# Second pass of a channel attention and dilated attention kernel: q of two groups in quarters of TensorE, in banks shared with the position taps, and two scaled taps summed by accumulating transfers

## The chip, the cores and the metric

The kernel runs on one core of a Trainium2 chip, in float32 with a few bfloat16 operands. The metric is the device time of one execution in microseconds (us), the median of several. The engines are called as in the profile: PE (TensorE matmuls), PEld (its weight loads), DVE (VectorE), ACT (ScalarE), POOL (GpSimd), SP (SyncE, which here only issues transfers).

## What is computed

The input `x` is 4 images of 192 channels and 128 x 128 pixels. Layer 0 is a channel attention: it ends in a per-channel mix of `v`, a gate and `x`, projected by a 1x1 convolution. Layer 1, which the change touches, takes the result `x` and does:

```python
pe = conv3x3_depthwise(x, pos_w)                  # nine taps a channel
x = x + pe + pos_b
qkv = einsum('oc,bchw->bohw', qkv_w, x)           # 192 -> 576 channels
# three groups of 64 channels (2 heads of 32), dilation 1, 2, 3:
scores = einsum('bnpd,bnpdk->bnpk', q, k_3x3)     # nine neighbours, reflected at the edges
attn = softmax(scores * 32**-0.5)
out_g = einsum('bnpk,bnpkd->bnpd', attn, v_3x3)
out = einsum('oc,bchw->bohw', proj_w, concat(out_1, out_2, out_3))
```

## The kernel before

There are three stages: a projection of `x` (`project`), the channel attention's matrices (`channel_attention`), and the second pass (`second_pass`), which does the last product of layer 0 and all of layer 1. Only the second pass is changed.

It works on blocks `n` of 4 image rows of two images at once: 64 blocks, of 512 pixels per image. Channels 0 to 127 of the two images lie in two tiles side by side, `hboth` (128 partitions, rows, 2 images, width); channels 128 to 191 of both images share one tile of 128 partitions, 64 for each (`HALVES`). For a block, in order:

- `h_product` (L803) and `h_evict` (L807): the output of layer 0 goes into rings of rows, `hboth` and `hring[2]`.
- The position taps of the first 128 channels: `centre` (L846) has ACT write the middle tap with the bias into the PSUM tile `pa` (two banks, one buffer), seven taps on DVE add to it (`tap`, L858; one operand is `hboth`, the other is `pa`), the last of them writes `y` in SBUF. The ninth tap, number 3, is scaled by ACT (`moved`, L870) and added to `y` by POOL (`moved_sum`, L875).
- The same taps for the last 64 channels: nine scaled copies on ACT (`side`, L882), added row by row by two accumulating transfers that POOL issues (`side_rows`, L894), and then by two POOL additions (L902, L905) into `y2`.
- `kv_product` (L945, L948) multiplies keys and values; ACT copies them into rings of rows, `kring` and `vring` (`kv_evict`, L958), with the reflected edges (`reflect`, L962, L963).
- `query` gives q of one group at a time in the bank `q` (one buffer): first two matmuls of 128x64 side by side (L1003, one for each image, which land in the two halves of the partitions), then one of 128x128 (L1000) whose weights `wq2` hold the 64-channel matrix twice on the diagonal and zeros elsewhere.
- `prod` (L1011) on DVE multiplies q with three windows of the key ring at a time, nine of them for a block; `pick_sums` (L1022) sums over the 32 channels of a head on PE; then the softmax (L1065 to L1110), whose weights a transposing transfer (L1110) turns.
- `expand` (L1146) spreads the weights over channels on PE into two banks, `term` (L1152) multiplies them with the value ring on DVE, `term_sum` (L1155) adds up on POOL, with four buffers for terms; `out_product` (L1164, L1168), `out_evict` (L1171) and `store` end the block.

The order of all instructions on every engine is computed when the kernel is built. `Schedule` keeps a list of operations, each with an engine, a rank (a due time in blocks), an estimated cost in us, what it comes after, a latency to other engines and, for PE, the shape of its setting. `hold` says that a buffer is taken by one operation and free after others, with as many in use at once as the pool has buffers. `order` then simulates the engines: a free engine takes the ready operation of lowest rank. The result is a fixed order in which each engine runs its instructions on the chip, waiting at each for what it needs. A changed cost, rank or buffer count therefore changes the written order of everything.

PSUM has eight banks: `pc` 2, `ex` 2, `q` 1, `pa` 2 (one tile), `sc` 1.

The planning of q and its products reads:

```python
t0 = n + 4.65
for g in range(NG):
    a = add("PE", t0 + (NT * g + 0.1) / 27, 0.86, (query, n, g, 0), [y[2]], COLS)
    b = add("PE", t0 + (NT * g + 0.11) / 27, 0.86, (query, n, g, 1), [a] + y[3], FULL)
    for ty in range(3):
        op = add("DVE", t0 + (NT * g + 3 * ty + 0.5) / 27, 1.75, (prod, n, g, ty), [b])
    hold("q", a, *mine)
```

Here `y[2]` is the finished `y`, `y[3]` that and `y2`.

Of the kernel before, what the change touches and what calls it, by code (L numbers as in the profile page):

```python
# [19 lines left out]
G = 64  # L20
NG = 3
# [13 lines left out]
class Schedule:  # L35
# [9 lines left out]
    def add(self, engine, rank, cost, run, after=(), shape=None, latency=LATENCY):  # L45
        op = dict(engine=engine, rank=rank, cost=cost, run=run, shape=shape, latency=latency, seq=len(self.ops))
        op.update(after=list(after), first=[], users=[], issued=[])
        self.ops.append(op)
        return op

    def hold(self, pool, bufs, first, last):

        self.pools.setdefault((pool, bufs), []).append((first, last))
# [130 lines left out]
    return t.rearrange("p (r w) -> p r w", w=W)  # L184


FULL, COLS, ROWS, QUADS = "128x128", "128x64", "64x128", "128x32"
HALVES = [slice(0, G), slice(G, 128)]
EXTRA = 2 * B * CH0 + B
SM = EXTRA + B * 2 * CH0  # L190
XV = 8
GATE = "wl wl2 dwl fc1T bfc1 fc2T bfc2 eye wprojT".split()
SECOND = "wp1 wq1 wq2 wkv wkv2 wo wo2 posw posb pick order spread".split()
AROUND = (0, 1, 2, 6, 7, 8, 3, 5)


# [550 lines left out]
def second_pass(tc, x, w2, xv_p, mix1, mix2, biases, v_dram, v2_dram, out):  # L747
# [4 lines left out]
    with ExitStack() as ctx:  # L752
# [3 lines left out]
            tc,  # L756
            "p2",
            dict(
                xv=XV, y=3, y2=3, prod=3, middle=2, side=1, moved=1, term=4, acc=4, o=3, s_sb=1, e=2, mx=2, sm=2, e_sb=2,
            ),  # L760
            dict(pc=2, ex=2, q=1, pa=1, sc=1),
            dict(xv=xv_p),
        )
        add, hold, tile_of, tiles = stage.schedule.add, stage.hold, stage.tile, stage.tiles
# [74 lines left out]


        by_row = lambda a: a.rearrange("p r b w -> p (r b) w")

        def centre(n):
            at = n * RB % RING
            to, of = tile_of("pa", ("pa", n), (128, RB, 2, W)), hboth[:, at : at + RB, :, 1 : W + 1]
            nc.scalar.activation(  # L846
                by_row(to), by_row(of), AF.Identity, bias=posb[:, 0:1], scale=posw[:, 0, 4:5]
            )
# [15 lines left out]
                    ALU.add,  # L864
                )

        def moved(n, t):
            to = tile_of("moved", ("moved", n), (128, RB, 2, W))
            at = n * RB % RING
            nc.scalar.activation(  # L870
                by_row(to), by_row(hboth[:, at : at + RB, :, t % 3 : t % 3 + W]), AF.Copy, scale=posw[:, 0, t : t + 1]
            )

        def moved_sum(n):
            nc.gpsimd.tensor_add(tiles["y", n], tiles["y", n], tiles.pop(("moved", n)))  # L875

        def side(n, ty, tx):

# [28 lines left out]
        def plan_conv(n):  # L907
            prev = first = add("ACT", n + 2, 1.25, (centre, n), latency=0.3)
            for m in range(2):
                read("h", m, n, 0, first)  # L910
            for j, t in enumerate(AROUND[:7]):
                prev = add("DVE", n + 2 + (j + 0.9) / 8, 1.28, (tap, n, t, j == 6), [prev])
                for m in range(2):
                    read("h", m, n, t // 3 - 1, prev)
            hold("pa", first, prev)
            two = prev
            mv = add("ACT", n + 2.5, 1.2, (moved, n, AROUND[7]))
            for m in range(2):
                read("h", m, n, 0, mv)
            both = add("POOL", n + 2.9, 2.4, (moved_sum, n), [mv, two])  # L920
            hold("moved", mv, both)
            firsts, sums = {}, []
            for j, ty in enumerate((1, 0, 2)):
                for tx in range(3):
                    sd = add("ACT", n + 2 + 0.3 * j + 0.08 * tx, 0.72, (side, n, ty, tx), firsts.get(ty, [])[-1:])
                    read("h", 2, n, ty - 1, sd)
                    firsts.setdefault(ty, []).append(sd)
                if j:
                    after = [firsts[1][-1], firsts[ty][-1], *sums[-1:]]
                    sums.append(add("POOL", n + 2.25 + 0.3 * j, 1.2, (side_rows, n, ty), after, latency=6.0))  # L930
                    hold("side", firsts[ty][0], sums[-1])
# [23 lines left out]
        def kv_evict(n, pair, im, e, kind, g):  # L955

            _, _, rows, pad = ring_rows(n, kind, g)
            nc.scalar.copy(rows[HALVES[im], :, pad : pad + W], rows3(tiles["pkv", n, pair, im])[HALVES[e]])  # L958

        def reflect(n, kind, g):  # L960
            _, _, rows, pad = ring_rows(n, kind, g)
# [31 lines left out]
            for at, length, o in runs(n, dy, size, True):  # L993
                yield ring[g][:, at : at + length, dx : dx + W], slice(o * W, (o + length) * W)

        def query(n, g, j):

            q = tile_of("q", ("q", n, g)) if j == 0 else tiles["q", n, g]
            if j:
                mm(q, wq2[:, g, :], tiles["y", n, 2], start=False, stop=True)  # L1000
                return
            for im in range(2):
                mm(rows3(q[HALVES[im]]), wq1[:, g * G : (g + 1) * G], tiles["y", n, im], start=True, stop=False)  # L1003

        def prod(n, g, ty):

# [23 lines left out]
        def plan_scores(n, y):  # L1030
            t0 = n + 4.65
            prods, used, picks = [], [], []
            for g in range(NG):
                a = add("PE", t0 + (NT * g + 0.1) / 27, 0.86, (query, n, g, 0), [y[2]], COLS)
                b = add("PE", t0 + (NT * g + 0.11) / 27, 0.86, (query, n, g, 1), [a] + y[3], FULL)
                used += [a, b]
                mine = []
                for ty in range(3):
                    op = add("DVE", t0 + (NT * g + 3 * ty + 0.5) / 27, 1.75, (prod, n, g, ty), [b])
                    read("k", g, n, (ty - 1) * (g + 1), op)  # L1040
                    mine.append(op)
                hold("q", a, *mine)
                prods += mine
            for row in range(7):
                of = prods[4 * row // 3 : min(4 * row + 3, NG * NT - 1) // 3 + 1]
                op = add("PE", of[-1]["rank"] + (2.5 + 0.1 * row) / 27, 0.86, (pick_sums, n, row), of, QUADS)
                op["after"] += picks[-1:]
                picks.append(op)
            for k, op in enumerate(prods):
                hold("prod", op, picks[(3 * k + 2) // 4])  # L1050
            return used, picks
# [131 lines left out]
        def plan_mixed(n, w):  # L1183
            t0 = n + 6.1
            sums, spreads = [], []
            for g in range(NG):
                exs, prev = [], None
                for t in range(NT):
                    u = t0 + (NT * g + t) / 27
                    exs.append(add("PE", u - 0.6 / 27, 0.25, (expand, n, g, t), [w], FULL))  # L1190
                    tm = add("DVE", u + 0.7 / 27, 0.62, (term, n, g, t), exs[-1:])
                    read("v", g, n, (t // 3 - 1) * (g + 1), tm)
                    hold("ex", exs[-1], tm)
                    if t == 0:
                        first = prev = tm
                        continue
                    prev = add("POOL", u + 1.2 / 27, 1.27, (term_sum, n, g, t), [tm, prev])
                    hold("term", tm, prev)
                spreads += exs
                sums.append((first, prev))  # L1200
            hold("e_sb", w, *spreads)
            used = []
            for m in range(2):
                ops = []
                for g in range(NG):
                    after = [sums[g][1]] + ops[-1:]
                    ops.append(
                        add(
                            "PE",
                            n + 7.25 + 0.07 * m + 0.01 * g,  # L1210
                            0.86,
                            (out_product, n, m, g),
                            after,
                            FULL if m else ROWS,
                        )
                    )
# [28 lines left out]
def _shapes_only():  # L1245
# [6 lines left out]
    pick[np.arange(128), QR + np.arange(128) // HD1] = 1  # L1252
    order = np.zeros((128, NS), f)
    for col in range(NS):
        order[col // 4 % 4 * 32 + col // 16 * 4 + col % 4, col] = 1
    spread = np.zeros((3, NT, 4, NT, 4, HD1), f)
    for t in range(NT):
        for h in range(4):
# [117 lines left out]
```

## Time and profile before

| | us |
|---|---|
| time, median of 3 runs (lowest to highest) | 4568.01 (4566.82 to 4569.73) |
| the profiled execution's own time | 4564.56 |
| its span, first to last instruction | 4562.7 |
| busy: PE, DVE, POOL, ACT | 4416.8, 3907.4, 3354.2, 2506.2 |

The stages can be told apart in the busy tenths: up to about 840 us the projection, up to about 1650 the channel attention, then the second pass, which is even from about 1800 to 4400 us and drains at the end. A row of a group gives its line, engine and operation, output and inputs, sizes, count, then busy us, mean ns of one, and the idle time of the engine ahead of it with what ended it. A float32 matmul appears as two records. The clock granted to TensorE was 0.987 of full speed over the span, and 1.00 in the even part of the second pass. Nearly all records of an even stretch are there; a few per cent of the matmuls and some other records are missing.

### The profile page before, as it was taken

The page shows a single profiled execution, that of the slowest core. Times are in us where ns is not written, and L with a number is a line of the kernel's source. Part 1 is how long each engine was busy: PE and PEld are TensorE (multiplying, and loading weights), DVE is VectorE, ACT ScalarE, POOL GpSimd, SP SyncE. Part 2 cuts the span into 40 slices and gives each one's busy share as a digit, 9 for nine tenths or more (in the row PEclk, how much of TensorE's full clock was granted, in tenths as well). Part 3 has the DMA queues.
Part 4 walks back from the last instruction along what each step waited for, and adds up shares of the span by engine and source line. Part 5 has one row for each costly group of instructions (what it writes and reads, how often), then busy time and mean ns, then how long its engine had stood idle before and what let it go on. Part 6 is the DMA issues. An engine that isn't in the chain of part 4 may idle for free.

```text
span 4562.7 us, 64190 instructions
## 1 busy us (share of the span) xinstructions
PE 4416.8 (97%) x20608; PEld 1602.8 (35%) x20608; DVE 3907.4 (86%) x5556; ACT 2506.2 (55%) x4794; POOL 3354.2 (74%) x3343
## 2 busy tenths in 40 slices
PE   9999999899999989999999999999999999999986
PEld 3333333345544532333333333333333333333321
DVE  7998889755455547899999999999999999999996
ACT  7888888633233345555555555555555555555531
POOL 6777788611111115888989999998998989999897
PEclk9999999999999989999999999999999999999997
DMA  8777787678677734443444443444434444344311
GB/s 271 241 242 232 244 256 242 192 164 178 150 167 169 167 89 97 99 99 97 101 98 93 105 103 91 106 96 101 101 90 108 98 100 101 92 109 99 78 44 28
DMA packets 483951, 608.93 MB, mean 133 GB/s; under 512 B 136528, under 2 KB 318364, under 8 KB 483616
## 3 DMA queue, kind: packets, MB, share of 16 engines
q1 hardware_dynamic: 464160, 504.94, 40.6%
q0 software_dynamic: 19456, 99.89, 11.3%
q8 instruction: 166, 2.72, 0.3%
q14 instruction: 169, 1.38, 0.1%
HBM read 277.72 MB, written 201.33 MB: 105 GB/s over the span
## 4 chain that ended last, share of the span: by engine, by line
PE 71%; DVE 14%; issue 6%; POOL 6%; DMA 2%; ACT 1%; POOLq 0%; SPq 0%; DVEq 0%; ACTq 0%
PE pc L576 11%; PE ph L803 9%; PE pu L293 7%; PE ex L1146 6%; PE sc L1022 6%; DVE prod L1011 5%; DVE term L1152 5%; POOL acc L1155 4%; PE pu L298 4%; PE gram L648 4%; PE po L1168 3%; PE po L1164 3%; PE pkv L945 3%; PE pu L426 2%; PE q L1000 2%
## 5 line engine op out<-in xcount | busy, mean ns | idle before, releaser
L1155 POOL TENSOR_TENSOR acc<-acc,term 128x512 f32<-128x512 f32 x1536 | 1977.4, 1289 | 211.9 <-DVE term L1152 135.5
L1152 DVE TENSOR_TENSOR term<-ex,vring 128x512 f32<-128x512 f32 (+2 forms) x1596 | 1007.3, 661 | 65.8 <-PE ex L1146 38.9
L1011 DVE TENSOR_TENSOR prod<-q,kring 128x1536 f32<-128x1536 f32 (+1 forms) x600 | 1008.3, 1686 | 31.7 <-ACT kring L963 13.8
L363 POOL TENSOR_TENSOR v_True<-v_True,side 128x512 f32<-128x512 f32 (+1 forms) x512 | 647.9, 1267 | 168.8 <-ACT side L352 141.1
L340 DVE SCALAR_TENSOR_TENSOR pa<-vboth,dwv,pa 128x1024 f32<-128x1024 f32 (+1 forms) x448 | 574.3, 1282 | 76.8 <-ACT pa L333 54.3
L1146 PE MATMUL ex<-e_sb,spread 108*128 108x512 bf16 x1728 | 596.2, 387 | 45.2 <-DVE acc L1152 21.3
L858 DVE SCALAR_TENSOR_TENSOR pa<-hboth,posw,pa 128x1024 f32<-128x1024 f32 (+1 forms) x384 | 489.5, 1275 | 59.0 <-ACT pa L846 45.1
L576 PE MATMUL pc<-u,band 64*64 64x508 f32 (+1 forms) x4608 | 517.5, 590 | 1.4 <-ACT ring L322 1.4
L563 POOL COPY band<-band 64x384 f32<-64x384 f32 x192 | 96.7, 504 | 561.3 <-DMA band<-in_bands 484.8
L1022 PE MATMUL sc<-prod,pick 128*32 128x512 f32 x3456 | 484.1, 607 | 4.1 <-DVE e L1079 2.8
L589 DVE BATCH_NORM_STATS2 stats<-pc 128x6 f32<-128x128 f32 x1440 | 303.3, 283 | 141.3 <-ACT conv L585 141.1
L1146 PEld LDWEIGHTS <-spread 108*128 108x128 bf16 x1728 | 149.0, 98 | 723.7 <-issue 692.2
L945 PE MATMUL pkv<-y,wkv 128*128 128x512 f32 x768 | 389.0, 618 | 8.1 <-ACT kring L958 2.5
L882 ACT ACTIVATE side<-hring,posw 128x512 f32<-128x512 f32 x512 | 335.2, 710 | 102.1 <-DMA side<-side 79.8
L803 PE MATMUL ph<-xv,mix 128*128 128x512 f32 (+1 forms) x1024 | 383.4, 606 | 5.4 <-DMA xv<-v_dram 4.9
L585 ACT COPY conv<-pc 128x512 f32<-128x512 f32 x384 | 211.4, 587 | 295.4 <-PE pc L576 288.8
L293 PE MATMUL pu<-xt,wx 128*128 128x512 f32 x768 | 365.3, 612 | 7.6 <-DMA xt<-in_x 7.6
L352 ACT ACTIVATE side<-ring,dwv 128x512 f32<-128x512 f32 (+1 forms) x512 | 350.6, 736 | 15.1 <-POOL v_True L363 14.3
L958 ACT COPY kring<-pkv 64x512 f32<-64x512 f32 x384 | 223.2, 581 | 221.7 <-PE pkv L948 210.5
L576 PEld LDWEIGHTS pc<-u,band 64*64 64x64 f32 x4608 | 188.4, 133 | 302.3 <-issue 282.1
L1171 ACT COPY o<-po 128x512 f32<-128x512 f32 x192 | 106.2, 588 | 304.5 <-PE po L1164 203.8
L958 ACT COPY vring<-pkv 64x512 f32<-64x512 f32 x384 | 223.4, 582 | 45.4 <-PE pkv L948 35.7
(164 smaller groups left out, 5961.0 us busy)
## 6 DMA issues: line engine op xcount, KB each, us to landing
qk_dram<-us SPq DMA_DIRECT2D x192, 512.0 KB
u<-qk_dram SPq DMA_DIRECT2D x384, 256.0 KB
side<-side POOLq DMA_DIRECT2D x124, 768.0 KB, 5.8
xt<-in_x SPq DMA_DIRECT2D x64, 512.0 KB
v_dram<-v_False SPq DMA_DIRECT2D x64, 512.0 KB
xv<-in_x SPq DMA_DIRECT2D x128, 256.0 KB
xv<-v_dram SPq DMA_DIRECT2D x128, 256.0 KB
out<-o SPq DMA_DIRECT2D x128, 256.0 KB
```

The costliest lines, as they stand in the source:

```text
L293: mm(pu, wx[:, mt * 128 : (mt + 1) * 128], tiles["xt", n][:, im, :], start=True, stop=False)
L340: nc.vector.scalar_tensor_tensor(by_row(to[:, o : o + length]), by_row(vboth[:, at : at + length, :, t % 3 : t % 3 + W]), dwv[:, 0, t : t ...
L363: nc.gpsimd.tensor_add(v[:, rows, :], v[:, rows, :], z[:, rows, :])
L576: nc.tensor.matmul(pcs[e][r * G : (r + 1) * G, :, to], band[at, e, c, dx, :], u[at, e, c, :].rearrange("p (b w) -> p b w", w=W)[:, :, of], ...
L803: mm(to, w[:, cols], tiles["xv", n, j, im], start=j == 0, stop=j == 2)
L858: nc.vector.scalar_tensor_tensor(by_row(to[:, o : o + length]), by_row(hboth[:, at : at + length, :, t % 3 : t % 3 + W]), posw[:, 0, t : t ...
L945: mm(rows3(tile_of("pc", key)), w, tiles["y", n, im], start=True, stop=False)
L1011: nc.vector.tensor_mul(to[:, :, px].rearrange("p t (r w) -> p t r w", w=W), q.unsqueeze(1).to_broadcast([128, 3, *q.shape[1:]]), three,)
L1022: mm(sc[quad * 32 : (quad + 1) * 32, :], pick[:, QR - 4 * row : QR - 4 * row + 32], tiles["prod", n, k // NT, k % NT // 3][:, k % 3, :], s ...
L1146: mm(rows3(tile_of("ex", ("ex", n, g, t))), spread[:, t, :], e_sb, start=True, stop=True)
L1152: nc.vector.tensor_mul(rows3(to[:, px]), rows3(ex[:, px]), win)
L1155: nc.gpsimd.tensor_add(tiles["acc", n, g], tiles["acc", n, g], tiles.pop(("term", n, g, t)))
```

## The change

- **q of groups 0 and 1 together.** `query` now takes a list of groups. For groups 0 and 1 it makes one PSUM tile of two banks. Its first half is four matmuls of 128x64. Its second half no longer uses the zero-padded 128x128 weights: four matmuls of 64x64, one for each image and group, each in its own quarter of the array. For this, group 1 has its images in exchanged halves (`SWAPPED`, `place`): in q, in `kring[1]`, and in the order of heads of the constant `order`. Group 2 is done as before in the bank `q`.
- **Shared banks.** The two-bank tile of the taps, `pa`, is now the pool `two`, with one buffer, which the taps and q of groups 0 and 1 take in turn. PSUM stays at eight banks.
- **Six taps on DVE, two on ACT.** Taps 3 and 8 are scaled by ACT into the two halves of `moved` (one buffer, twice as large). POOL issues an accumulating transfer of tap 8 onto tap 3, and, after the last DVE tap has written `y`, a second one of their sum onto `y`. The POOL addition goes. `y` has four buffers for three.
- **Planned numbers.** A tap costs 1.22 for 1.28, a product 1.69 for 1.75 with a latency of 0.4 for 0.2, an expansion 0.23 for 0.25; the taps are due 0.075 of a block apart for 0.125, and the scaled taps at the start of the block.

```diff
-                xv=XV, y=3, y2=3, prod=3, middle=2, side=1, moved=1, ...
+                xv=XV, y=4, y2=3, prod=3, middle=2, side=1, moved=1, ...
-            dict(pc=2, ex=2, q=1, pa=1, sc=1),
+            dict(pc=2, ex=2, q=1, two=1, sc=1),
...
+SUMMED, MOVED, TAPS = (0, 1, 2, 6, 7, 5), (3, 8), 0.075
+        place = lambda im, g, kind="k": HALVES[im ^ (g == SWAPPED and kind == "k")]
...
-        def moved_sum(n):
-            nc.gpsimd.tensor_add(tiles["y", n], tiles["y", n], tiles.pop(("moved", n)))
+        def moved_sum(n, k):
+            reach = runs(n, MOVED[1 - k] // 3 - 1, RING, False)
+            flat = lambda a: a[:, reach[0][2] : reach[-1][2] + reach[-1][1]].rearrange("p r b w -> p (r b w)")
+            of = tiles["moved", n]
+            nc.gpsimd.dma_start(flat(tiles["y", n] if k else of[:, 0]), flat(of[:, 1 - k]), accum_op=ALU.add)
...
-            for j, t in enumerate(AROUND[:7]):
-                prev = add("DVE", n + 2 + (j + 0.9) / 8, 1.28, (tap, n, t, j == 6), [prev])
+            for j, t in enumerate(SUMMED):
+                prev = add("DVE", n + 2 + TAPS * (j + 0.9), 1.22, (tap, n, t, j == 5), [prev])
...
-            hold("pa", first, prev)
-            mv = add("ACT", n + 2.5, 1.2, (moved, n, AROUND[7]))
-            both = add("POOL", n + 2.9, 2.4, (moved_sum, n), [mv, two])
-            hold("moved", mv, both)
+            hold("two", first, prev)
+            for k, t in enumerate(MOVED):
+                mvs.append(add("ACT", n + 2.0 + 0.05 * k, 1.15, (moved, n, k, t), mvs[-1:]))
+            both = add("POOL", n + 2.2, 0.85, (moved_sum, n, 0), mvs, latency=6.0)
+            both = add("POOL", n + 2.6, 0.85, (moved_sum, n, 1), [both, two], latency=6.0)
+            hold("moved", mvs[0], both)
...
+        def query(n, groups, j):
+            if j == 0:
+                t = tile_of("two" if len(groups) == 2 else "q", ("q", n, *groups), (128, len(groups), PX))
+                for k, g in enumerate(groups):
+                    tiles["q", n, g] = t[:, k, :]
+            for g in groups:
+                q = tiles["q", n, g]
+                if j and len(groups) == 1:
+                    mm(q, wq2[:, g, :], tiles["y", n, 2], start=False, stop=True)
+                    continue
+                for im in range(2):
+                    if j == 0:
+                        w, of = wq1[:, g * G : (g + 1) * G], tiles["y", n, im]
+                        mm(rows3(q[place(im, g)]), w, of, start=True, stop=False)
+                    else:
+                        w, of = wq2[HALVES[im], g, HALVES[im]], tiles["y", n, 2][HALVES[im]]
+                        mm(q[place(im, g)], w, of, start=False, stop=True)
...
+            for groups in ((0, 1), (2,)):
+                t1 = t0 + NT * groups[0] / 27
+                a = add("PE", t1 + 0.1 / 27, 1.0 * len(groups), (query, n, groups, 0), [y[2]], COLS)
+                second = QUARTERS if len(groups) == 2 else FULL
+                b = add("PE", t1 + 0.11 / 27, 0.86, (query, n, groups, 1), [a] + y[3], second)
...
+                        op = add("DVE", u, 1.69, (prod, n, g, ty), [b], latency=0.4)
...
+                hold("two" if len(groups) == 2 else "q", a, *mine)
```

More of the change, by code (lines that the diff above doesn't have):

```diff
@@ L184, in rows3 @@
     return t.rearrange("p (r w) -> p r w", w=W)
-FULL, COLS, ROWS, QUADS = "128x128", "128x64", "64x128", "128x32"
+FULL, COLS, ROWS, QUADS, QUARTERS = "128x128", "128x64", "64x128", "128x32", "64x64"
 HALVES = [slice(0, G), slice(G, 128)]
+SWAPPED = 1
 EXTRA = 2 * B * CH0 + B
@@ L758, in second_pass @@
             dict(
-                xv=XV, y=3, y2=3, prod=3, middle=2, side=1, moved=1, term=4, acc=4, o=3, s_sb=1, e=2, mx=2, sm=2, e_sb=2,
+                xv=XV, y=4, y2=3, prod=3, middle=2, side=1, moved=1, term=4, acc=4, o=3, s_sb=1, e=2, mx=2, sm=2, e_sb=2,
             ),
-            dict(pc=2, ex=2, q=1, pa=1, sc=1),
+            dict(pc=2, ex=2, q=1, two=1, sc=1),
             dict(xv=xv_p),
@@ L841, in second_pass @@
         by_row = lambda a: a.rearrange("p r b w -> p (r b) w")
+        place = lambda im, g, kind="k": HALVES[im ^ (g == SWAPPED and kind == "k")]
         def centre(n):
             at = n * RB % RING
-            to, of = tile_of("pa", ("pa", n), (128, RB, 2, W)), hboth[:, at : at + RB, :, 1 : W + 1]
+            to, of = tile_of("two", ("pa", n), (128, RB, 2, W)), hboth[:, at : at + RB, :, 1 : W + 1]
             nc.scalar.activation(
@@ L865, in tap, with moved @@
                 )
[L867 to L872, printed above, removed]
-        def moved_sum(n):
-            nc.gpsimd.tensor_add(tiles["y", n], tiles["y", n], tiles.pop(("moved", n)))
+        def moved(n, k, t):
+            to = tile_of("moved", ("moved", n), (128, 2, RB, 2, W)) if k == 0 else tiles["moved", n]
+            for at, length, o in runs(n, t // 3 - 1, RING, False):
+                nc.scalar.activation(
+                    by_row(to[:, k, o : o + length]),
+                    by_row(hboth[:, at : at + length, :, t % 3 : t % 3 + W]),
+                    AF.Copy,
+                    scale=posw[:, 0, t : t + 1],
+                )
+        def moved_sum(n, k):
[3 more added lines that the diff above has]
+            nc.gpsimd.dma_start(flat(tiles["y", n] if k else of[:, 0]), flat(of[:, 1 - k]), accum_op=ALU.add)
         def side(n, ty, tx):
@@ L910, in plan_conv @@
                 read("h", m, n, 0, first)
-            for j, t in enumerate(AROUND[:7]):
-                prev = add("DVE", n + 2 + (j + 0.9) / 8, 1.28, (tap, n, t, j == 6), [prev])
+            for j, t in enumerate(SUMMED):
+                prev = add("DVE", n + 2 + TAPS * (j + 0.9), 1.22, (tap, n, t, j == 5), [prev])
                 for m in range(2):
                     read("h", m, n, t // 3 - 1, prev)
-            hold("pa", first, prev)
-            two = prev
-            mv = add("ACT", n + 2.5, 1.2, (moved, n, AROUND[7]))
-            for m in range(2):
-                read("h", m, n, 0, mv)
-            both = add("POOL", n + 2.9, 2.4, (moved_sum, n), [mv, two])
-            hold("moved", mv, both)
+            hold("two", first, prev)
+            two, mvs = prev, []
+            for k, t in enumerate(MOVED):
+                mvs.append(add("ACT", n + 2.0 + 0.05 * k, 1.15, (moved, n, k, t), mvs[-1:]))
+                for m in range(2):
+                    read("h", m, n, t // 3 - 1, mvs[k])
+            both = add("POOL", n + 2.2, 0.85, (moved_sum, n, 0), mvs, latency=6.0)
+            both = add("POOL", n + 2.6, 0.85, (moved_sum, n, 1), [both, two], latency=6.0)
+            hold("moved", mvs[0], both)
             firsts, sums = {}, []
@@ L957, in kv_evict @@
             _, _, rows, pad = ring_rows(n, kind, g)
-            nc.scalar.copy(rows[HALVES[im], :, pad : pad + W], rows3(tiles["pkv", n, pair, im])[HALVES[e]])
+            nc.scalar.copy(rows[place(im, g, kind), :, pad : pad + W], rows3(tiles["pkv", n, pair, im])[HALVES[e]])
         def reflect(n, kind, g):
@@ L994, in windows @@
                 yield ring[g][:, at : at + length, dx : dx + W], slice(o * W, (o + length) * W)
[L996 to L1003, printed above, removed]
+        def query(n, groups, j):
[15 more added lines that the diff above has]
+                        mm(q[place(im, g)], w, of, start=False, stop=True)
         def prod(n, g, ty):
@@ L1032, in plan_scores @@
             prods, used, picks = [], [], []
-            for g in range(NG):
-                a = add("PE", t0 + (NT * g + 0.1) / 27, 0.86, (query, n, g, 0), [y[2]], COLS)
-                b = add("PE", t0 + (NT * g + 0.11) / 27, 0.86, (query, n, g, 1), [a] + y[3], FULL)
+            for groups in ((0, 1), (2,)):
[3 more added lines that the diff above has]
+                b = add("PE", t1 + 0.11 / 27, 0.86, (query, n, groups, 1), [a] + y[3], second)
                 used += [a, b]
                 mine = []
[L1038 to L1042, printed above, removed]
+                for g in groups:
+                    for ty in range(3):
+                        u = t0 + (NT * g + 3 * ty + 0.5) / 27
+                        op = add("DVE", u, 1.69, (prod, n, g, ty), [b], latency=0.4)
+                        read("k", g, n, (ty - 1) * (g + 1), op)
+                        mine.append(op)
+                hold("two" if len(groups) == 2 else "q", a, *mine)
                 prods += mine
@@ L1189, in plan_mixed @@
                     u = t0 + (NT * g + t) / 27
-                    exs.append(add("PE", u - 0.6 / 27, 0.25, (expand, n, g, t), [w], FULL))
+                    exs.append(add("PE", u - 0.6 / 27, 0.23, (expand, n, g, t), [w], FULL))
                     tm = add("DVE", u + 0.7 / 27, 0.62, (term, n, g, t), exs[-1:])
@@ L1254, in _shapes_only @@
     for col in range(NS):
-        order[col // 4 % 4 * 32 + col // 16 * 4 + col % 4, col] = 1
+        head = col % 4 ^ 2 * (col // GT == SWAPPED)
+        order[col // 4 % 4 * 32 + col // 16 * 4 + head, col] = 1
     spread = np.zeros((3, NT, 4, NT, 4, HD1), f)
```

## The prediction

> **What bounds the kernel now.** I read the busy table by stage first, because the page's shares average three different stages. Only the second pass (from about 1700 us to the end) is touched. Its even stretch, 2536.2 to 3978.8 us, holds 33 blocks: the group of the moved tap's sum on POOL (L875) counts 33 and starts once in a block. So a block takes 1442.6 / 33 = 43.71 us.
>
> ```profile
> 2536.20:3978.80 1442.60, 1428.52 (x5712) 460.12 (x5708) 1403.16 (x1599) 778.37 (x1577) 1308.25 (x1055) 1.00 0.42 100
> L858 DVE SCALAR_TENSOR_TENSOR pa<-hboth,posw,pa 128x1024 f32<-128x1024 f32 x192 | 246.4, 1283 | 16.4 <-ACT pa L846 15.2
> L1003 PE MATMUL q<-y,wq 128*64 128x512 f32 x396 | 106.7, 617 | 0.6 <-DVE prod L1011 0.5
> L1000 PE MATMUL q<-y,wq 128*128 128x512 f32 x198 | 101.2, 592 | 0.0
> L875 POOL TENSOR_TENSOR y<-y,moved 128x1024 f32<-128x1024 f32 x33 | 78.3, 2374 | 0.0
> L894 POOL DMA_DIRECT2D side<-side x66 | 57.7, 874 | 0.0
> L870 ACT ACTIVATE moved<-hboth,posw 128x1024 f32<-128x1024 f32 x33 | 37.9, 1150 | 56.2 <-POOL y L875 56.2
> ```
>
> The first line gives busy us of PE, weight loads, DVE, ACT and POOL, then clock, DMA share and GB/s. Over 33: PE 43.29, DVE 42.52, ACT 23.59, POOL 39.64 us a block, DMA 0.42. PE and DVE are both full; POOL has 4.1 us to spare. The chain of waits confirms it: within one block it runs some 30 us on PE back to back (3004 to 3034 us), then some 14 us on DVE, and changes over again.
>
> Busy time overstates PE, so I went on to PE's timeline:
>
> ```profile
> 3004.24 0.38 PE L1146 MATMUL ex<-e_sb,spread 108*128 108x512 bf16 x1 [0.30 <-DVE acc L1152]
> ...
> 3035.04 1.08 PE L1003 MATMUL q<-y,wq 128*64 128x512 f32 x4
> 3036.05 0.60 PE L1146 MATMUL ex<-e_sb,spread 108*128 108x512 bf16 x2
> 3036.49 1.02 PE L1000 MATMUL q<-y,wq 128*128 128x512 f32 x2
> 3037.35 1.88 PE L945 MATMUL pkv<-y,wkv 128*128 128x512 f32 x4
> ...
> 3042.77 2.33 PE L945 MATMUL pkv<-y,wkv 128*128 128x512 f32 x4
> ```
>
> One float32 matmul is two records. From start to next start: the pair of 128x64 matmuls takes 1.01 us, the 128x128 one 0.86. The first line stood 0.30 us waiting for DVE to free an expansion bank, and the last took 0.45 us more than its like. So PE has 43.71 - 0.30 - 0.45 = 42.96 us of work, DVE 42.52, and 0.75 us is lost where the two wait for each other.
>
> **What the Trainium skill says.** "TensorEngine Tiling (Array Packing)", Tiling Modes, says a 64x64 setting is four independent tiles and that a change of mode drains the engine. The trace agrees with both. The channel attention stage already runs four 64x64 matmuls together:
>
> ```profile
> 1299.57 12.99 PE L576 MATMUL pc<-u,band 64*64 64x508 f32 x120
> ```
>
> 120 records are 60 matmuls, 15 sets of four: 0.87 us a set, the price of one whole matmul. The drain shows as the 0.15 us by which the 128x64 pair exceeds 0.86. "DMA: Bandwidth & Descriptors", Anatomy of one DMA, estimates 2.0 us plus bytes over 436 GB/s; for the 786,432 bytes of one side_rows transfer that is 3.8 us. The trace says otherwise, 5.8 us from issue to landing, so I use the trace. "SBUF — State Buffer", Who interferes with whom, says transfers issued by POOL suffer when DVE holds the port it shares with POOL, and that a DVE instruction with at most one SBUF input leaves it alone. The taps, products and terms here have one operand in PSUM, and the 68 issues looked at lasted 0.842 to 1.286 us, median 0.860: no such stall shows.
>
> **Part by part, per block.**
>
> *q of groups 0 and 1 together.* Removed: two pairs and two whole matmuls, 2 x (1.01 + 0.86) = 3.74 us. Added: four 128x64 matmuls in one run, 1.01 + 0.86 = 1.87, and one set of quarters, 0.87 plus a drain of 0.13 = 1.00. Saved 0.87 us. Group 2 stays. If the planner puts an expansion between the two runs, one more drain costs 0.1; if joining them removes one, 0.1 is gained: 0.77 to 0.97. All lies on PE, one of the two paths that set the period. The swap of k's halves in group 1 changes which half a copy writes and the values of a constant: no instruction more or less.
>
> *Six taps on DVE for seven.* A tap lasts 1.28 (246.4 / 192), but in DVE's timeline the next instruction starts 1.19 us after it (3036.09 to 3037.28) and 1.25 if that is the following tap (two from 3044.67 to 3047.18). Saved 1.20 us, on the other path.
>
> *A second scaled tap on ACT.* +1.15 us (L870), ACT 23.6 to 24.7 of 43.7: hidden by ACT's idle half. The wait to look at is the 1.7 us a block in which it stands for the one moved buffer (56.2 / 33). The buffer is now held until the second transfer lands: scale 2.3, two transfers, and the taps; with waits some 20 us of 43, so it should be free in time. Behind it on ACT stand key and value copies and the h copies that PE waits for; cost 0, bounds -0.2 to +1.0 us.
>
> *The sum by two accumulating transfers.* Off POOL: 2.37 us. On POOL: two issues. An issue lasts 0.87, but the next instruction starts 0.62 after it (3026.89 to 3027.51). POOL saves 0.63 to 1.13 us. On the DMA engines:
>
> ```profile
> 3003.00:3004.00 1.00, 0.94 (x4) 0.15 (x3) 1.00 (x2) 0.99 (x2) 0.00 (x0) 1.00 0.97 197
> 3004.00:3005.00 1.00, 0.76 (x3) 0.47 (x3) 1.00 (x3) 0.95 (x3) 0.12 (x1) 1.00 1.01 197
> 3005.00:3006.00 1.00, 1.00 (x8) 0.26 (x9) 0.90 (x2) 0.98 (x6) 1.00 (x1) 1.00 0.98 197
> ```
>
> A side_rows transfer fills all 16 engines for four microseconds at 197 GB/s. The new ones are 524,288 bytes each: 2.66 us, and from issue to landing 5.8 - 4.0 + 2.7 = 4.5 us. DMA goes from 0.42 to 0.42 + 2 x 2.66 / 43 = 0.54. The last scattered load is the transposed softmax weights: issued at 3037.4, moved by 3041.4, and the first expansion near 3045, a margin of some 3.5 us; one new transfer in the way (2.7) stays inside it, two would not.
>
> *y later after its last tap.* Now last tap to y is 3.4 us (tap ends 3014.3, sum ends 3017.7); then an issue behind a running POOL sum plus 4.5, so 5 to 6. PE's first key product of that y is the one at 3037.35 by the order in which the pc banks are taken (its four copies into the key rings follow): some 20 us later. Two microseconds vanish in that. A fourth y buffer holds what is kept longer.
>
> *Shared banks.* The two banks of the taps are now also those of q of groups 0 and 1. Taps follow products and products follow taps, each through a wait. No row shows this; rival B prices it. Gone in exchange: one of three waits of q's single bank a block.
>
> *Planned costs* (1.69, 1.22, 0.23, a latency of 0.4 and the spacing of the taps) move only the written order; their effect is part of the lost 0.75 us.
>
> **Sum.** PE 42.96 - 0.87 = 42.09, DVE 42.52 - 1.20 = 41.32, POOL about 38.8. If 0.75 us is lost as before, the period is 42.84, 0.87 less. From where the pass is full (about 1800 us) to where it drains (about 4410) are 60 periods, and the ramps hold some two more: 62 x 0.87 = 54 us. The drain hangs on POOL's sums of the last blocks (L1155), untouched. The profiled execution took 4564.56 us (span 4562.7), 3.5 below the median of 4568.01; 4510.6 for it, 4514 for the median. If the loss falls to 0.3, as DVE is now 0.77 below PE instead of 0.44, 28 us more: 4486. If it grows to 1.2: 4542.
>
> **Rivals.**
>
> *A, as above:* 4514, 4486 to 4542. For it: both full engines lose work and no full one gains any. Chance 0.59.
>
> *B, slower: the shared banks make a loop.* Centre on ACT 1.2 and its wait 0.5, six taps 7.2, q on PE 2.9 behind whatever PE is running (up to 2.8), six products 10.1: 22 to 25 us with 17.3 of DVE in it. The other 24 us of DVE work must fill the 5 to 8 us in which the loop is on ACT or PE. Terms can only run four ahead of POOL (four buffers, 1.29 us each there) and two ahead of PE (two expansion banks). DVE idles 43.71 - 42.52 = 1.19 us a block now; this decides once it idles over 43.71 - 41.32 = 2.4 us. At 3.0 us the period is 44.3: 62 x 0.6 = 37 us slower, 4605. For it: ACT's centre already makes DVE wait 0.46 us a block (15.2 / 33), and every engine runs in its written order, so a misjudged duration stops all behind it. Against: the loop needs just over half a period. Chance 0.28.
>
> *C, no gain: POOL blocks.* The second transfer waits on POOL for the first's landing and for the last tap; the term sums queue behind it, and then DVE, out of term buffers. POOL's spare 4.9 us has to be used up. With PE and DVE each losing about 0.9 us to it the time stays within 0.2% of 4568. Chance 0.10.
>
> *D, the quarters don't run side by side:* a set would take 1.7 and PE saves nothing; DVE alone wins little: 4568 to 4560. L576 speaks against it. Chance 0.03.
>
> **Numbers.** A measurement of this kernel can tell about 0.2%, 9 us, from no change. A is faster throughout; B slower, less a small part of mild cases; C and D mostly same. Faster 0.60, same 0.10, slower 0.30. The range leaves out the far ends of A and B: 4482 to 4612; within A alone 4486 to 4542.
>
> **What would show it.** Right: a period near 42.8 us between first scaled taps; q's second half for two groups at about 1.0 us as 64x64 matmuls; six tap records on DVE a block for seven, DVE near 41.3 us a block; POOL near 38.8; transfers landing in about 4.5 us; DMA share 0.54. B: DVE idle before the first tap or the first product over 2.4 us, released by ACT pa or PE q. C: POOL idle before its transfers, released by DVE or DMA. My forecast is wrong if PE is idle over 1.6 us a block, whatever ends it.

## The result, and the profile after

The changed kernel took 4751.53 us (median of 4 runs, 4748.89 to 4754.67) against 4567.41 for the kernel before on the same chip: a ratio of 1.0403, interval 1.0385 to 1.0421, 184 us slower. I had forecast 4514 and a range up to 4612.

The second pass is even again from 2126.8 to 4196.7 us and holds 44 blocks there, by the copies of the scores (L1093, once a block). A block takes 47.04 us; by the same count 47 blocks of the kernel before took (4164.0 - 2105.0) / 47 = 43.81. The difference of 3.23 over some 60 blocks is an estimated 194 us, about the whole loss.

First the view of busy time by stretch of the kernel after: its even stretch, and one block of it cut in three (PE, weight loads, DVE, ACT, POOL, then clock, DMA share, GB/s).

```profile
2126.80:4196.70 2069.90, 1919.59 (x7771) 624.63 (x7772) 1823.00 (x2069) 1084.03 (x2142) 1724.66 (x1452) 0.97 0.51 115
3081.00:3095.00 14.00, 13.87 (x61) 4.07 (x62) 13.40 (x15) 10.06 (x24) 8.65 (x8) 1.00 0.60 125
3095.00:3110.00 15.00, 12.37 (x45) 4.03 (x44) 11.19 (x13) 5.09 (x12) 14.37 (x13) 0.89 0.24 61
3110.00:3128.00 18.00, 17.57 (x79) 6.13 (x76) 16.46 (x20) 9.75 (x14) 16.82 (x16) 1.00 0.71 159
```

Over 44, PE is busy 43.63 us a block, DVE 41.43, POOL 39.20: none fills 47.04. The cut block shows a hole that wanders. In the first 14 us POOL is busy 8.65; in the next 15 PE and DVE miss 2.6 and 3.8 us, and PE's clock is down to 0.89. So the hole begins on POOL.

Then the groups of the same stretch. The first eight lines answer to those shown of before, the last three are where the idle time stands.

```profile
L861 DVE SCALAR_TENSOR_TENSOR pa<-hboth,posw,pa 128x1024 f32<-128x1024 f32 x215 | 274.8, 1278 | 1.0
L1024 PE MATMUL q<-y,wq 128*64 128x512 f32 x528 | 130.5, 601 | 0.0
L1019 PE MATMUL q<-y,wq 128*128 128x512 f32 x88 | 49.5, 645 | 0.0
L1027 PE MATMUL q<-y,wq 64*64 64x512 f32 x344 | 46.8, 615 | 0.0
L886 POOL DMA_DIRECT2D moved<-moved x44 | 38.2, 867 | 3.4 <-ACT moved L874 2.3 <-ACT parts L1123 0.6
L886 POOL DMA_DIRECT2D y<-moved x44 | 38.0, 864 | 0.0
L905 POOL DMA_DIRECT2D side<-side x88 | 90.4, 1027 | 0.0
L874 ACT ACTIVATE moved<-hboth,posw 128x1024 f32<-128x1024 f32 x86 | 98.9, 1150 | 46.2 <-DMA y<-moved 44.8
...
L913 POOL TENSOR_TENSOR y<-side 128x512 f32<-128x512 f32 x44 | 55.7, 1265 | 222.4 <-DMA side<-side 129.0 <-PE ex L1174 67.1 <-PE po L1196 26.3
L1180 DVE TENSOR_TENSOR term<-ex,vring 128x512 f32<-128x512 f32 x1039 | 687.3, 683 | 230.7 <-POOL acc L1183 155.0 <-PE ex L1174 69.5 <-PE st L1100 5.3
L1174 PE MATMUL ex<-e_sb,spread 108*128 108x512 bf16 x1185 | 421.8, 393 | 144.2 <-DVE term L1180 135.7 <-DMA e_sb<-parts 0.3 <-DVE acc L1180 0.2
```

What I had suspected is clean: the tap into the shared banks stood 1.0 us in all, the two new transfers 3.4 us. The idle time is at the y2 addition (`side_sum`, L913): 222.4 / 44 = 5.05 us a block. It needs the second `side_rows` transfer, by then the instruction just ahead of it on POOL. (A part is put down to PE, but there too the addition starts mostly 5.9 us after the issue, as when the transfer is named.) The timeline of one such place in the kernel before, on POOL:

```profile
3045.33 0.86 POOL L894 DMA_DIRECT2D side<-side  x1
3048.56 2.62 POOL L1155 TENSOR_TENSOR acc<-acc,term 128x512 f32<-128x512 f32 x2 [2.37 <-DVE term L1152]
3051.18 1.28 POOL L902 TENSOR_TENSOR y<-side 128x512 f32<-128x512 f32 x1
```

The transfer lands while POOL waits for a term and adds it up: two sums and a wait that was there anyway cover it. The same place in the kernel after, on POOL, then DVE, then PE:

```profile
3081.50 6.70 POOL L1183 TENSOR_TENSOR acc<-acc,term 128x512 f32<-128x512 f32 x5
3088.15 0.86 POOL L905 DMA_DIRECT2D side<-side  x1
3094.05 1.26 POOL L913 TENSOR_TENSOR y<-side 128x512 f32<-128x512 f32 x1 [5.04 <-DMA side<-side]
...
3093.76 0.68 DVE L1180 TENSOR_TENSOR term<-ex,vring 128x512 f32<-128x512 f32 x1
3097.90 0.69 DVE L1180 TENSOR_TENSOR term<-ex,vring 128x512 f32<-128x512 f32 x1 [3.46 <-POOL acc L1183]
...
3095.00 1.02 PE L1192 MATMUL po<-acc,wo 128*128 128x512 f32 x2
3098.64 0.58 PE L1174 MATMUL ex<-e_sb,spread 108*128 108x512 bf16 x1 [2.63 <-DVE term L1180]
```

POOL issues and then stands for the landing; the term sums queue behind; DVE fills its four term buffers and stands; PE fills its two expansion banks and stands. POOL's account closes on the period, in us a block: 39.20 busy, 5.05 before L913, 0.98 for a softmax sum, 1.65 before term sums (0.21 of it for DVE, the rest small gaps), 0.16 elsewhere: 47.04. The block grew by 3.23 us and not by 5.05: in the kernel before POOL was busy 39.70 us a block, and so idle 4.11, of which 2.2 were for terms (102.6 / 47).

### The profile page after: what moved, and what is told of

It reads as the page before. It is cut to its first block, busy times and chain, and to the rows that moved or that the text cites. A ratio compares the mean times of both kernels' runs of the same rounds, so it can differ in the third digit from the quotient of the medians.

```text
span 4752.9 us, 65025 instructions
## 1 busy us (share of the span) xinstructions
PE 4449.6 (94%) x20864; PEld 1619.2 (34%) x20864; DVE 3840.1 (81%) x5492; ACT 2577.7 (54%) x4858; POOL 3323.0 (70%) x3407
## 3 DMA queue, kind: packets, MB, share of 16 engines
q14 instruction: 172, 1.41, 0.1%
## 4 chain that ended last, share of the span: by engine, by line
PE 55%; POOL 19%; DVE 10%; issue 7%; DMA 7%; ACT 1%; POOLq 0%; SPq 0%; DVEq 0%; ACTq 0%
POOL acc L1183 14%; PE pc L578 11%; PE pu L295 7%; DMA side<-side 6%; PE ph L805 5%; PE ex L1174 4%; PE pu L300 4%; PE gram L650 4%; PE pkv L958 4%; DVE term L1180 3%; PE sc L1046 3%; DVE prod L1035 3%; PE pu L428 2%; PE q L1024 2%; POOL y L916 2%
## 5 line engine op out<-in xcount | busy, mean ns | idle before, releaser
L1183 POOL TENSOR_TENSOR acc<-acc,term 128x512 f32<-128x512 f32 x1536 | 2034.5, 1325 | 124.3 <-DVE term L1180 33.3
L1180 DVE TENSOR_TENSOR term<-ex,vring 128x512 f32<-128x512 f32 (+2 forms) x1596 | 1019.0, 662 | 332.7 <-POOL acc L1183 212.3
L1174 PE MATMUL ex<-e_sb,spread 108*128 108x512 bf16 x1728 | 617.7, 395 | 211.0 <-DVE term L1180 190.9
L861 DVE SCALAR_TENSOR_TENSOR pa<-hboth,posw,pa 128x1024 f32<-128x1024 f32 (+1 forms) x320 | 406.7, 1271 | 38.4 <-ACT pa L849 23.6
L958 PE MATMUL pkv<-y,wkv 128*128 128x512 f32 x768 | 413.2, 663 | 4.2 <-ACT hring L809 3.4
L805 PE MATMUL ph<-xv,mix 128*128 128x512 f32 (+1 forms) x1024 | 399.5, 606 | 5.4 <-DMA xv<-v_dram 4.9
L1174 PEld LDWEIGHTS <-spread 108*128 108x128 bf16 x1728 | 138.8, 98 | 726.5 <-issue 695.4
L913 POOL TENSOR_TENSOR y<-side 128x512 f32<-128x512 f32 x64 | 81.3, 1270 | 320.5 <-DMA side<-side 211.4
```

What stands on the lines that cost most here:

```text
L805: mm(to, w[:, cols], tiles["xv", n, j, im], start=j == 0, stop=j == 2)
L861: nc.vector.scalar_tensor_tensor(by_row(to[:, o : o + length]), by_row(hboth[:, at : at + length, :, t % 3 : t % 3 + W]), posw[:, 0, t : t ...
L958: mm(rows3(tile_of("pc", key)), w, tiles["y", n, im], start=True, stop=False)
L1174: mm(rows3(tile_of("ex", ("ex", n, g, t))), spread[:, t, :], e_sb, start=True, stop=True)
L1180: nc.vector.tensor_mul(rows3(to[:, px]), rows3(ex[:, px]), win)
L1183: nc.gpsimd.tensor_add(tiles["acc", n, g], tiles["acc", n, g], tiles.pop(("term", n, g, t)))
```

## The experiments

Why is that addition there? `order` makes a user ready by this line, in all kernels of the case:

```python
release(o, end + op["latency"] * (o["engine"] != engine))
```

The latency of a transfer counts for other engines only. To POOL's own next instructions its transfer looks landed as soon as it is issued. In the kernel before, two term sums stood between transfer and addition in 40 of 50 planned blocks; in the changed one nothing does, in 49 of 50.

| kernel | time, us | ratio to before, interval | us a block |
|---|---|---|---|
| e1, after, y2 additions later | 4561.92 | 0.9984, 0.9978 to 0.9991 | 43.61 |
| e2, after, latency counted on POOL | 4555.16 | 0.9972, 0.9962 to 0.9982 | 43.95 |
| e3, before, four y2 buffers | 4748.33 | 1.0394, 1.0377 to 1.0412 | 47.26 |
| e4, e1 with six term buffers | 4507.89 | 0.987, 0.9854 to 0.9886 | 42.69 |
| e5, e2 with weights ahead of loads | 4502.81 | 0.986, 0.9845 to 0.9875 | 42.87 |
| e6, e5 with six term buffers | 4500.07 | 0.9852, 0.9838 to 0.9867 | 42.76 |
| e7, before, six term buffers | 4554.5 | 0.9968, 0.9958 to 0.9979 | 43.66 |
| e8, e6 without q's part | 4712.96 | 1.0316, 1.0299 to 1.0333 | 46.59 |
| e9, e6 without the taps' part | 4541.15 | 0.9942, 0.9928 to 0.9957 | 43.86 |

**e1: the order of POOL alone.** The two y2 additions come five term sums later; the orders of PE, DVE, ACT and SP are those of the changed kernel, line for line.

```diff
-            for op in self.schedule.order():
+            for op in later(self.schedule.order(), 5 * ("moved" in self.bufs)):
```

> The changed kernel with one thing moved: on POOL, the two y2 additions (L913, L916) of each block come after five further term sums instead of right behind the second side_rows transfer that they wait for. The order of PE, DVE, ACT and SP is unchanged, line for line. Theory T1 (POOL stands 5.0 us a block at L913 for the landing of a transfer it has just issued): the wait is covered by five sums of 1.29 us, the period falls from 47.0 us to between 42.8 and 43.5, the time to 4515-4560 us. Theory T2 (shared banks, the added transfers or a lower clock cost the time, and L913 only shows it): POOL's wait moves elsewhere and the time stays at 4700-4760.

4561.92: the loss of 184 us is gone, and 6 us more. POOL's timeline shows the same place, with work between:

```profile
3049.02 0.88 POOL L905 DMA_DIRECT2D side<-side  x1
3052.07 6.67 POOL L1183 TENSOR_TENSOR acc<-acc,term 128x512 f32<-128x512 f32 x5 [2.18 <-DVE term L1180]
3058.70 1.27 POOL L913 TENSOR_TENSOR y<-side 128x512 f32<-128x512 f32 x1
```

The addition no longer waits at all. Nothing but the place of two instructions a block was changed, so that place is the loss. POOL again stands for a term here (2.18 us), as in the kernel before. The time is just above the range expected: a further gain is still missing, see e4.

**e3: the same loss without the change.** If the place alone does it, the kernel before must show it too. Its y2 addition is held back because there are three y2 buffers; with a fourth the planner puts it directly behind the transfer in 45 of 50 blocks.

```diff
-                xv=XV, y=3, y2=3, prod=3, ...
+                xv=XV, y=3, y2=4, prod=3, ...
```

> The kernel before with a fourth y2 buffer and nothing else: the planner, which no longer sees the y2 addition wait for a buffer, then puts it right behind the second side_rows in most blocks (45 of 50 planned ones), where before two term sums stood between. T1: POOL waits about 5 us a block here too, and the kernel before becomes slower by 2 to 3.5 us a block, 4690-4790 us. T2: a buffer more and no other part of the change: within 0.5% of the kernel before, 4545-4590.

4748.33, within 4 us of the changed kernel, by giving a buffer. The same row of the view of waits, for the even stretch of the kernel before and then for e3:

```profile
POOL y L902 <- DMA side<-side: 12.4, 13, 5.0
```

```profile
POOL y L902 <- DMA side<-side: 215.9, 44, 5.7
```

Columns: us in all, times, longest. 13 waits became 44, one in each block, of 4.9 us. Quarters, shared banks, new transfers and planned costs of the change are all absent here. The fourth buffer moves more than that addition: from about block 27 on the orders of PE, DVE and ACT differ too. But from block 9 to block 25 those of DVE, ACT and SP are the kernel before's, and PE's but for five exchanges of near neighbours; there a block already takes 48.3 us (16 blocks by the copies of the scores, 2164.6 to 2937.9 us) for 43.7 (2152.0 to 2851.5). So POOL's order makes the loss here too.

**e2, e5, e6: mending the rule.** e2 counts a latency over 1 us for the own engine too.

```diff
-                    release(o, end + op["latency"] * (o["engine"] != engine))
+                    release(o, end + op["latency"] * (o["engine"] != engine or op["latency"] > 1))
```

> The changed kernel with the planner mended: the latency of a transfer (6.0 us) also counts for a later operation on the engine that issued it, so the whole order is planned anew; nine term sums then stand between the second side_rows and the y2 addition. T1: as e1, 4510-4550 us, and TensorE's granted clock back to 1.00. T2: 4700-4760.

4555.16, some 5 us above the range expected. Eight term sums and the issue of a new transfer now stand between transfer and addition in 49 of 50 blocks, and in those the POOL wait is gone; but every engine got a new order, a block takes no less than before (43.95 us for 43.81), and a new wait came: `ex` (L1174) for the transposed softmax weights, 51.9 us in 31 places from 2100 to 4200 us. SP's queue in the timeline shows why:

```profile
3683.04 2.85 SPq L792 DMA_DIRECT2D xv<-in_x  x2
3685.99 2.69 SPq L1138 DMA_TRANSPOSE e_sb<-parts  x1
```

The softmax's last step on POOL (L1133) had ended by 3684.1; the transposing transfer stood behind a run of row loads that nothing yet needed. e5 puts these loads behind it.

```diff
-            for op in self.schedule.order():
+            for op in weights_first(self.schedule.order(), 80 * ("moved" in self.bufs)):
```

> e2 with one thing moved: on SP the eight loads of x and v of a block come behind the transposing transfer of the softmax weights instead of ahead of it; the order of PE, DVE, ACT and POOL is unchanged. In e2 the transfer was issued some 2 us late behind those loads, landed 6 us later among them, and PE stood 1.1 us a block for it. Theory T5 (DMA traffic and the SP queue hold the weights up): the wait goes, the period falls by 0.6 to 1.2 us, 4480-4520 us. Rival T6 (the loop is held by POOL, and PE's wait only shows it): below 0.2% of change, 4545-4560 us.

4502.81: the wait for `e_sb` is gone but for one place of 3.4 us, and 52 us with it. e6 gives this order six term buffers; a y buffer goes for their room.

```diff
-                xv=XV, y=4, ... term=4, ...
+                xv=XV, y=3, ... term=6, ...
```

> e5 with six term buffers for four and three y buffers for four. T3: a further 0.3 to 0.8 us a block below e5, 4450-4500 us. T4: as e5 within 0.2%.

4500.07, 2.7 us less than e5 and within what can be told from none. So T4 holds here, and not T3: in this order four buffers nearly suffice. It is the fastest of the case, 1.5% under the kernel before.

**e4 and e7: term buffers.** e1 leaves PE idle for 43.61 - 42.22 = 1.39 us a block, the kernel before for 43.81 - 43.29 = 0.52. e4 keeps e1's order, but for 12 PE instructions of the drain, and has six term buffers for four (and three y for four, for room).

> e1 with six term buffers for four (and three y buffers for four, to make room; the planned order of every engine is that of e1). In e1 DVE stood 1.8 us a block for a term buffer that POOL had not freed, while POOL stood 2.4 us for DVE at other places. Theory T3 (what is left of the forecast gain is lost where DVE and POOL wait for each other through four term buffers): these waits go, the period falls by 0.5 to 1.0 us, 4500-4530 us. Rival T4 (the loss comes from somewhere else, such as the weights' transposing transfer or ACT waiting for the moved buffer): 4550-4565 us.

4507.89. The rows of the view of waits, from 2100 to 4200 us, of e1 and then of e4:

```profile
DVE term L1180 <- POOL acc L1183: 84.8, 138, 0.9
PE ex L1174 <- DVE term L1180: 52.7, 127, 1.0
```

```profile
DVE term L1180 <- POOL acc L1183: 11.6, 28, 0.7
PE ex L1174 <- DVE term L1180: 17.6, 64, 0.5
```

DVE hardly stands for a free term now, and PE's wait falls to a third. The busy view of e4's even stretch, 49 blocks:

```profile
2105.30:4197.10 2091.80, 2059.00 (x8656) 676.63 (x8657) 2018.81 (x2299) 1210.91 (x2385) 1916.20 (x1616) 1.00 0.56 126
```

42.69 us a block, PE busy 42.02 and so idle 0.67, DVE busy 41.20, POOL 39.11, DMA 0.56. Is that gain the change's, or was it open to the kernel before? e7 gives the kernel before six term buffers.

> The kernel before with six term buffers for four and nothing else (the planned order stays). T3 (the term buffers hold the changed kernel only, since its DVE makes terms faster than POOL clears them): DVE waits 0.1 us a block for a term buffer in the kernel before, so its time stays within 0.2%, 4558-4577 us. Rival T7 (more term buffers help any version, and the gain of e4 is not the change's): 4510-4540 us.

4554.5, 14 us faster, between what the two theories said. But the order did not stay: with six buffers the planner wrote PE, DVE, ACT and POOL anew up to about block 22. The lead is gained there, and nothing is added where the order is again that of the kernel before. Block 24 comes 11.6 us earlier (copy of its scores at 2796.2 us for 2807.8), block 56 12.0 us earlier (4196.1 for 4208.1), so a block takes 43.75 and 43.76 us in between. At an equal order, six buffers bring the kernel before nothing, as T3 said; the 54 us from e1 to e4 belong to the changed kernel.

**e8 and e9: one part at a time**, both in the form of e6. e9 keeps the joined q and goes back to seven taps on DVE and POOL's sum.

```diff
-SUMMED, MOVED, TAPS = (0, 1, 2, 6, 7, 5), (3, 8), 0.075
+SUMMED, MOVED, TAPS = (0, 1, 2, 6, 7, 8, 3), 5, 0.075
...
-            both = add("POOL", n + 2.2, 0.85, (moved_sum, n, 0), mvs, latency=6.0)
-            both = add("POOL", n + 2.6, 0.85, (moved_sum, n, 1), [both, two], latency=6.0)
+            both = add("POOL", n + 2.6, 2.4, (moved_sum, n), [mv, two])
```

> q's part alone (groups 0 and 1 in quarters of TensorE, in the banks shared with the taps), seven taps on DVE and the eighth summed by POOL as in the kernel before; planner, SP order and six term buffers as in e6. PE falls to 42.1 us of work a block and DVE keeps 42.5. T8: 4530-4562 us. Rival T10 (PE was the bound, and q brings nearly all): 4500-4515 us.

4541.15, 27 us under before, in the range expected, but not by a shorter period: a block takes 43.86 us for 43.81, though PE is busy only 42.83 for 43.29. In the profiled executions e9 is 21.6 us ahead by block 8 (copy of its scores at 2083.4 us for 2105.0) and 17.3 by block 56 (4190.8 for 4208.1). So the lead is gained while the pass fills, under another order, and in the even stretch q's part alone shows no gain. From e9 to e6, whose edits differ in the taps' part alone (the orders follow from it), the block falls to 42.76 and the time by 41 us more. e8 drops q's part.

```diff
-SWAPPED = 1
+SWAPPED = -1
...
-            for groups in ((0, 1), (2,)):
+            for groups in ((0,), (1,), (2,)):
```

> The taps' part alone (six taps on DVE, two on ACT, two transfers), q as in the kernel before with its single bank for each group in turn; planner, SP order and six term buffers as in e6. PE keeps its 43.0 us of work a block and DVE falls to 41.2. Theory T8 (PE and DVE are both full, so neither part alone brings more than half of the gain of e6, which is 68 us): 4530-4562 us. Rival T9 (DVE was the bound, and the taps bring nearly all): 4500-4515 us.

4712.96, which no theory had. Its rows of the view of waits:

```profile
ACT side L893 <- DMA side<-side: 189.8, 44, 6.4
PE po L1192 <- ACT o L1199: 94.5, 42, 4.1
DVE pa L861 <- ACT pa L849: 57.4, 29, 3.6
```

Once a block ACT stands 4.3 us for the one `side` buffer, and PE and DVE then stand for ACT. It is another order with another misplaced wait, and says nothing clean about the taps' worth without q; T8 is left untested on that side. Which planned number brings that order about was not followed up and stays open.

## Why the prediction was wrong, point by point

**The step that failed** is "Planned costs ... move only the written order; their effect is part of the lost 0.75 us". A changed order was given no price of its own. In the changed kernel's order one addition stands directly behind the transfer it needs, which makes POOL stand 5.05 us a block and takes the period to 47.04 us for the 42.84 forecast; e1 takes the wait away by order alone, and e3 brings it about without the change. Which entries moved the addition was not tried one by one: the planned costs named in that sentence, the joined q, the new operations on POOL and the buffers all enter the planner. The price stood in the trace of the kernel before: the row of L902 shown above, from 2105 to 4164 us, says 13 waits, the longest 5.0 us. I had read 2500 to 4000 us, where the same row says 8 waits, 2.6 us in all, the longest 0.8. But my own 5.8 us from issue to landing was already the price of an addition right behind its transfer.

**Rival C** had the right chain (POOL blocks, term sums queue, DVE runs out of buffers), but at the new transfers, which wait 3.4 us in all over 44 blocks, and at a price of no gain. On its own terms one figure was lacking: 38.8 us of work and 5.05 of waiting are 43.85 on POOL, already more than the period of 42.84 forecast, before any small gaps.

**Rival B** did not come about: no tap or product waits for the shared banks to an extent that counts. **Rival D** neither: the timeline of e6 shows q of two groups as

```profile
3626.07 1.94 PE L1024 MATMUL q<-y,wq 128*64 128x512 f32 x8
...
3633.90 1.09 PE L1027 MATMUL q<-y,wq 64*64 64x512 f32 x8
```

The eight records of quarters are four matmuls, side by side: 1.09 us from first start to last end, where 1.00 to the next start was forecast; one after the other they would take an estimated four times 0.86. "TensorEngine Tiling (Array Packing)", on which that step rested, holds here. By busy time q falls from 6.30 us a block ((106.7 + 101.2) / 33) to 5.16 in e4 ((145.3 + 55.1 + 52.3) / 49), 1.1 for the 0.87 forecast from start to start.

**The sum** holds once the order does. e4: DVE 41.20 (41.32 forecast), DMA 0.56 (0.54), a period of 42.69 (42.84), 4507.89 us (4514). That it comes so close is in part luck: PE's busy time fell by 1.27 (43.29 to 42.02) where 0.87 of work were forecast, and it takes six term buffers, which the change doesn't have, or the order of e5. POOL is busy 39.1 us a block, not 38.8. And "lost as before" did not come by itself: by busy time PE is idle 0.52 us a block before, 1.39 in e1 with four term buffers, and 0.67 in e4. The buffer of the scaled taps, which "should be free in time", is not: ACT stands 2.6 us a block for it in e4 (128.6 / 49), more than the 1.7 before, at no price that shows. The forecast landing of 4.5 us for a new transfer was 4.6 for the second; the first, issued near the side transfers, took 6.5 in the middle, and nothing waited for it.

The sign of being wrong, "PE is idle over 1.6 us a block, whatever ends it", came: 3.4 us a block (47.04 - 43.63), 3.1 of it behind DVE (135.7 / 44).

## What to carry to other kernels

Where a planner writes the order, a change of costs or buffers is a change of order, and its price can be that of a wait elsewhere, as here and in e8: look in the views of waits, over the whole even stretch, for rows whose longest far exceeds the mean over blocks, and ask what it would cost if it came every time. A gain seen in the total can come from the filling of the pass alone, as in e7 and e9: compare periods where the order is the same. An engine that issues transfers and also computes must not be handed their consumer next; a planner has to count a transfer's latency for the issuing engine too. After mending one order, look at every other queue of the new one, SP's loads and the buffers that were just enough included.

## What the runs showed of the hardware

- **Waiting behind one's own transfer.** "DMA: Bandwidth & Descriptors", Rules for kernel authors, advises to issue early, compute, and wait late. Here is its price where it is not done: 5.0 us of standing a block for a transfer of 768 KB, 190 us in the kernel (4751.53 for e1's 4561.92).
- **The clock follows the stall.** "TensorE: Matmul & The Clock Gate", HAM oscillation, warns of pauses of PE over some 3.4 us. Here shorter ones went with a lower clock: in the even stretch of the kernel after, the clock was granted at half 29 times, for 3.4 or 6.8 us, and at 28 of them PE's longest pause, in the drop or in the 5 us ahead of it, was 1.7 to 2.6 us (once it was 4.3). What the throttle counts is not shown. The granted clock was 0.97 over the stretch, 0.89 in the 15 us cut out above, and 1.00 in e1 and e4. PE's busy time was 43.63 us a block, 42.22 in e1 with the same instructions, so of the 3.43 us between their periods 2.02 are pauses and 1.41 longer work.
- **POOL's own work grew.** With the new transfers two softmax additions took 1.29 and 1.18 us (L1127, L1133) for 1.02 each, a term sum 1.33 for 1.29, the side issues 1.03 for 0.87. Much the same in e1 and e4, so it isn't the stall. It is mostly the work close behind an issue that grew: in the stretch of the kernel after, a term sum right behind an issue took 1.74 us in the mean (88 of them) and one with no issue among the three instructions ahead 1.28 (789), a side issue right behind the one onto `y` 1.16 and the other 0.87. Why was not tried.
- **A transfer behind another lands later.** The first side transfer of a block, mostly issued 0.6 us behind the new one onto `y`, landed after 7.8 us in the middle, for 5.9 before. The second, for which the addition waits, landed after 5.75 as before.
